# Span attention with joint small operations and exponentials by head

## The chip, the cores and the metric

The kernel runs on one core of a Trainium2 chip. The time is the device time of one execution in microseconds (us); lower is better. A profile of one execution shows what each engine did: TensorE (PE, with weight loads as PEld), VectorE (DVE), ScalarE (ACT), GpSimd (POOL) and SyncE (SP), which issues transfers.

## What is computed

A block of three layers, each added to its input. Batch 32, 64 rows each, width 256, 16 heads; the context has 1601 keys.

```
x = x + xattn(layernorm(x), ctx, ctx, mask, ...)      # 16 heads over 1601 keys
x = x + span(layernorm(x), W_span, W_val, W_out)
x = x + ffn(layernorm(x), ...)                        # shared gated part + 2 of 8 experts

def span(h, W_span, W_val, W_out):                    # per batch and head, m = 64 rows
    s, value = heads(h @ W_span.T, 2), heads(h @ W_val.T, 16)
    mean = sigmoid(s[..., 0]) * m
    soft = softplus(s[..., 1])
    diff = arange(m) - mean[..., None]
    attn = softmax(-soft[..., None] * diff * diff)    # over the 64 positions
    return merge(attn @ value) @ W_out.T
```

The change touches the span layer only, and there `mean`, `soft` and the softmax.

## The kernel before

**The large loop.** The cross attention takes nearly all of the time. It goes through 64 halves (a half is 8 heads of one batch element); half n has four quarters g, one for each group of key chunks. In a quarter PE makes the scores of the next half (line 495), projects keys (line 450, evicted by ACT at line 465) and values (line 450, evicted at line 482) of the next batch element, and in the first and last quarter multiplies probabilities by values (line 571). DVE evicts each bank of scores while it adds the mask (line 504), and keeps a running maximum in the PSUM tile `mrun` (line 525); ACT writes the first block into `mrun` (line 517, `first_maxima`), DVE reduces the turned maxima at line 539, once a half. POOL subtracts the maxima (line 556, four to a half), once ACT has copied them out (line 551); ACT takes the exponentials (line 561, four to a half). Scores, keys and values share six PSUM banks: a matmul that wants a bank waits for the eviction of what was in it.

**The order.** PE, DVE, ACT and POOL run in exactly the order in which the program writes the instructions (a manual schedule), each engine in order. SP's order is left to the framework. Quarter g of half n is stretch 4n + g.

**Small work between.** The other layers' work for a tile of 128 rows (two batch elements, four halves; 16 tiles) is cut into steps by generators. `run(stretch)` takes the step that is due, and what it yields is the number of stretches until the next. `run` stands after the quarter's scores and projections, and before `first_maxima` or the quarter's exponential. `WAITS` holds the yields of `span_steps` for tiles 0 to 13, `CLOSE` those for tiles 14 and 15, whose span layers reach into the end of the program, where feed-forward units fill PE.

**The span layer's steps** (`span_steps`, lines 213 to 356). After projections, z = exp(-|s|) for both columns of s. Then the small chain, lines 279 to 295, 20 operations on DVE over 128 x 16 elements. With z0 and z1 the two columns: the sigmoid is max(z0, [s0 >= 0]) / (1 + z0). The softplus is max(s1, 0) + log(1 + z1), the logarithm as 2 atanh(z1 / (z1 + 2)), by a series in odd powers up to the 15th, six Horner steps (lines 291 to 294). Its temporaries `num`, `den`, `rat`, `atp`, `acc` are `held`, slices of `mrun` (`aside`, line 400), so ACT's copy at line 517 comes after the chain; `rden`, `at`, `twice`, `at2`, `mean`, `soft` lie in SBUF. In the next steps, on `sc`, 128 x 16 heads x 64 positions: POOL subtracts the mean from the position (line 300), ACT squares (304), POOL multiplies by `soft` (305), DVE takes each head's minimum `least` (308), POOL subtracts it (309), ACT takes exp(-x) of all 1024 elements (311), DVE sums each head to `total` (313) and takes the reciprocal (314), POOL multiplies (315). PE transposes the result (323) for the product with the values, and the sum goes on to `x_kept` and the feed-forward part.

For tile t the chain runs in the first quarter of a half with n mod 4 = 2, `least` in its last quarter, the exponential in the first quarter of the next half, the sum in its second.

Of the kernel before, what the change touches and what calls it, by code (L numbers as in the profile page):

```python
# [15 lines left out]
F32 = mybir.dt.float32  # L16
U8 = mybir.dt.uint8
AF = mybir.ActivationFunctionType
ALU = mybir.AluOpType
AX = mybir.AxisListType  # L20
PSUM = bass.MemoryType.PSUM

P = 128
S = 64
D = 256
H = 16
# [6 lines left out]
GROUPS = [(0, 4), (4, 3), (7, 3), (10, 3)]  # L33
BETWEEN = [(), (1, 2, 3), (4, 5, 6), (7, 8, 9), (10, 11, 12)]
LN_EPS = 1e-5
MASKED = -1e30
BIG = 3e38
E, TOPK, PRIME, HASH_OFF = 8, 2, 11, 7919
# [23 lines left out]
def shape_constants() -> np.ndarray:  # L62
# [5 lines left out]
    for e in range(2):  # L68
        c[:, C_OWN + e] = (row % 32) // 16 == e
    c[:, C_PAD] = np.where(row >= KEYS - (NKC - 1) * CHUNK, 2 * MASKED, 0.0)  # L70
    return c
# [3 lines left out]
def perceiver_kernel(ctx: ExitStack, tc: tile.TileContext, a: dict[str, bass.AP], out: bass.AP):  # L75
    nc = tc.nc
# [6 lines left out]
    const = ctx.enter_context(tc.tile_pool(name="const", bufs=1))  # L83
# [80 lines left out]

    neghalf = const.tile([P, 1], F32, name="neghalf")
    nc.gpsimd.memset(neghalf, -0.5)
    own4 = const.tile([P, 2], F32, name="own4")
    nc.vector.tensor_scalar(own4, own, 0.25, None, ALU.mult)

# [6 lines left out]
    def spread_of(src, name: str):  # L176
# [7 lines left out]
        ve = work.tile([P, 1], F32, tag="ve", bufs=4, name=f"ve_{name}")  # L184
        nc.vector.tensor_scalar(ve, mv[:, 1:2], LN_EPS, None, ALU.add)
        rstd = work.tile([P, 1], F32, tag="rstd", bufs=4, name=f"rstd_{name}")
# [3 lines left out]
    def normalised(src, spread, name: str):  # L190
        neg, rstd = spread
        xn = work.tile([P, D], F32, tag="xn", name=f"xn_{name}")
        nc.scalar.activation(xn, src, AF.Identity, bias=neg)
        nc.scalar.activation(xn, xn, AF.Copy, scale=rstd)
        return xn
# [11 lines left out]

    WAITS = (1, 1, 1, 1, 1, 1, 1, 1, 1, 1, 1, 3, 3, 1, 1, 1)  # L210
    CLOSE = (1, 1, 1, 1, 0, 2, 1, 1, 1, 1, 1, 2, 1, 1, 1, 1)

    def span_steps(t: int, oT):
        waits = iter(CLOSE if t >= NTILE - 2 else WAITS)
        x = xs[t]
# [8 lines left out]
        h = normalised(x, spread, f"h{t}")  # L224
# [12 lines left out]
        z = span_pool.tile([P, H, 2], F32, tag="z", name=f"z_{t}")  # L237
# [13 lines left out]
        for b in range(2):  # L251
            for c in range(2):
                for j in range(4):
                    e, i = divmod(j, 2)
# [13 lines left out]
        def small(tag: str):  # L268
            return span_pool.tile([P, H], F32, tag=tag, name=f"{tag}_{t}")
# [1 line left out]


        held = aside(f"held_{t}")
        num, den, rat, atp, acc = (held[:, i * H : (i + 1) * H] for i in range(5))
        s0, s1, z0, z1 = span[:, :, 0], span[:, :, 1], z[:, :, 0], z[:, :, 1]
        mean, soft, rden, at, twice, at2 = (
            small(n) for n in ("mean", "soft", "rden", "at", "twice", "at2")
        )
        nc.vector.tensor_scalar(rat, z1, 2.0, None, ALU.add)
        nc.vector.tensor_scalar(den, z0, 1.0, None, ALU.add)  # L280
        nc.vector.tensor_scalar(num, s0, 0.0, None, ALU.is_ge)
        nc.vector.reciprocal(rat, rat)
        nc.vector.reciprocal(rden, den)
        nc.vector.tensor_tensor(num, z0, num, ALU.max)
        nc.vector.tensor_tensor(atp, z1, rat, ALU.mult)
        nc.vector.tensor_tensor(at, z1, rat, ALU.mult)
        nc.vector.scalar_tensor_tensor(twice, z1, 2.0, rat, ALU.mult, ALU.mult)
        nc.vector.tensor_tensor(at2, at, atp, ALU.mult)
        nc.vector.scalar_tensor_tensor(mean, num, float(S), rden, ALU.mult, ALU.mult)

        nc.vector.tensor_scalar(acc, at2, 1.0 / 15, None, ALU.mult)
        for n in (13, 11, 9, 7, 5, 3):
            nc.vector.scalar_tensor_tensor(acc, acc, 1.0 / n, at2, ALU.add, ALU.mult)  # L293
        nc.vector.scalar_tensor_tensor(acc, acc, 1.0, twice, ALU.add, ALU.mult)
        nc.vector.scalar_tensor_tensor(soft, s1, 0.0, acc, ALU.max, ALU.add)  # L295
        yield next(waits)
# [1 line left out]
        full = [P, H, S]  # L298
        sc = span_pool.tile(full, F32, tag="sc", name=f"sc_{t}")
# [6 lines left out]
        yield next(waits)  # L306
        least, total = small("least"), small("total")
        nc.vector.tensor_reduce(least, sc, AX.X, ALU.min)  # L308
        nc.gpsimd.tensor_tensor(sc, sc, least[:, :, None].to_broadcast(full), ALU.subtract)
        yield next(waits)  # L310
        nc.scalar.activation(sc, sc, AF.Exp, scale=-1.0)
        yield next(waits)
        nc.vector.tensor_reduce(total, sc, AX.X, ALU.add)  # L313
        nc.vector.reciprocal(total, total)
        nc.gpsimd.tensor_tensor(sc, sc, total[:, :, None].to_broadcast(full), ALU.mult)
        yield next(waits)
# [2 lines left out]
        for q in range(2):  # L319
            ps = mm_bank(f"psa_{t}_{q}")  # L320
            for i in range(4):
                n = 4 * q + i
# [6 lines left out]
        for c in range(2):  # L329
            for b in range(2):  # L330
                for j in range(4):
                    n = 4 * c + j
# [32 lines left out]
    madd = big.tile([P, NKC, S], F32, name="madd", bufs=1)  # L365
    nc.vector.tensor_scalar(madd[:CHUNK], m8[:CHUNK], -MASKED, MASKED, ALU.mult, ALU.add)
    nc.vector.tensor_scalar(
# [271 lines left out]
    def finish_steps(b: int, stretch: int):  # L639

        t = b // 2
        if b % 2 == 0:
            oT[t] = work.tile([P, 2, 2, S], F32, tag="oT", name=f"oT_{t}")
        flat = "p c u r q -> p (c u r q)"
        nc.vector.transpose(turned_pvs.rearrange(flat), pvs.rearrange(flat))
        by_head = turned_pvs.rearrange("p c u r i -> p (c u r) i")
        rec = work.tile([P, 8], F32, tag="rec", name=f"rec_{b}")
        nc.vector.reciprocal(rec, by_head[:, :, DK])
        o = work.tile([P, 8, DK], F32, tag="o", name=f"o_{b}")
        nc.vector.tensor_tensor(  # L650
            o, by_head[:, :, :DK], rec[:, :, None].to_broadcast([P, 8, DK]), ALU.mult
        )
        nc.vector.transpose(oT[t][:, :, b % 2, :], o.rearrange("p (c n) i -> p c (n i)", c=2))
        if b % 2:
            agenda[stretch + 1].append(span_steps(t, oT.pop(t)))
        yield
# [266 lines left out]
```

## Time and profile before

| | us |
|---|---|
| median of 4 runs | 1606.19 |
| lowest and highest | 1604.48, 1607.47 |
| the profiled execution | 1606.7 |
| its span, first to last instruction | 1604.7 |

The granted clock of TensorE was 0.997 over the span. Some groups of the span layer, each 16 times in the program, once for a tile (the mean of one in us), and beside them the large loop's:

| line | engine | what | us each |
|---|---|---|---|
| 279 to 295 | DVE | the small chain, 20 operations | 0.16 to 0.27 each |
| 300, 305, 309, 315 | POOL | operations on 128 x 1024 | 1.90 |
| 308, 313 | DVE | minimum, sum over 128 x 1024 | 1.20, 1.21 |
| 304, 311 | ACT | square, exponential of 128 x 1024 | 1.05, 1.07 |
| 504 | DVE | eviction of scores, 16 to a half | 0.58 |
| 525 | DVE | running maximum, 11 to a half | 0.69 |
| 556 | POOL | subtraction of the maxima | 3.73 |
| 561 | ACT | exponential of 124 x 1664 | 1.59 |

How to read it: a busy share counts only executing instructions. A row of a timeline has the start in us from the span's beginning, how long it took, engine, line, operation, what it writes and reads, shape and count, and in brackets how long the engine had stood idle before it and what ended that. Neighbours on an engine may overlap by about a tenth of a microsecond, as an instruction's record ends when its writes are in.

### The profile page before, as it was taken

How to read it: one execution, taken by the hardware profiler on the slowest of the kernel's cores; microseconds unless marked ns; L12 is line 12 of the kernel's file. 1: busy time of each engine (PE TensorE's matmuls, PEld its weight loads, DVE VectorE, ACT ScalarE, POOL GpSimd, SP SyncE). 2: the span in 40 equal slices, each digit the busy share in tenths (PEclk: the TensorE clock that was granted, in tenths of full speed). 3: DMA queues.
4: the chain of work that ended last, by engine and by line, in shares of the span. 5: the costliest groups of instructions: out<-in, count | busy, mean ns of one | idle time of the engine just before them, and what ended most of it. 6: DMA issues, size and time to landing. Idle time of an engine off the chain costs nothing.

```text
span 1604.7 us, 62733 instructions
## 1 busy us (share of the span) xinstructions
PE 1531.8 (95%) x28600; PEld 1101.7 (69%) x28600; DVE 1261.3 (79%) x2700; ACT 897.1 (56%) x1229; POOL 1121.1 (70%) x424
## 2 busy tenths in 40 slices
PE   8999999999999999999999999999999999988899
PEld 5676676676767676676766676676767676654487
DVE  4888888888888988888888888888888988885200
ACT  3565656565565656555666556555656556555311
POOL 1777777778687877788686877688686977771610
PEclk9999999999999999999999999999999999999999
DMA  5111111111111111111111111111111111004100
GB/s 170 56 40 35 38 44 38 34 50 44 50 44 50 31 41 34 34 49 44 50 44 50 31 41 36 39 44 44 50 44 50 32 44 36 15 2 152 56 23 30
DMA packets 52072, 73.78 MB, mean 46 GB/s; under 512 B 3812, under 2 KB 51040, under 8 KB 51680
## 3 DMA queue, kind: packets, MB, share of 16 engines
q1 hardware_dynamic: 50992, 69.00, 15.1%
q8 instruction: 224, 3.67, 1.0%
q10 hardware_dynamic: 816, 0.79, 0.1%
q14 instruction: 40, 0.33, 0.1%
HBM read 65.57 MB, written 4.19 MB: 43 GB/s over the span
## 4 chain that ended last, share of the span: by engine, by line
PE 60%; DVE 36%; issue 2%; ACT 1%; DMA 1%; POOL 1%; ACTq 0%; SPq 0%; DVEq 0%; POOLq 0%
PE pv L450 13%; PE pk L450 13%; DVE mrun L525 13%; DVE prob L504 13%; PE pvs L571 9%; PE psc L495 9%; PE py L853 3%; PE u L600 3%; PE pm L532 2%; PE ph L835 2%; PE pb L547 1%; DVE total L313 1%; DVE least L308 1%; DVE mrun L293 1%; PE po L343 1%
## 5 line engine op out<-in xcount | busy, mean ns | idle before, releaser
L556 POOL TENSOR_TENSOR prob<-prob,mb 124x1664 f32<-124x1664 f32 x252 | 936.1, 3733 | 305.6 <-ACT mb L551 210.3
L504 DVE TENSOR_TENSOR prob<-psc,madd 124x384 f32<-124x384 f32 (+1 forms) x1024 | 582.4, 582 | 176.1 <-PE psc L495 176.0
L525 DVE TENSOR_TENSOR mrun<-prob,mrun 124x512 f32<-124x512 f32 x704 | 483.9, 687 | 6.6 <-ACT mrun L517 2.6
L450 PE MATMUL pk<-ct,wkT_sb 128*32 128x361 f32 (+2 forms) x1768 | 405.0, 499 | 15.2 <-DMA wkT_sb<-in_wkT 5.6
L561 ACT ACTIVATE prob<-prob 124x1664 f32<-124x1664 f32 x256 | 403.1, 1587 | 16.9 <-POOL prob L556 14.0
L450 PE MATMUL pv<-wvT_sb,ct 128*32 128x256 f32 (+3 forms) x4268 | 385.8, 379 | 0.0
L450 PEld LDWEIGHTS pv<-wvT_sb,ct 128*32 128x32 f32 (+3 forms) x4268 | 258.5, 123 | 128.8 <-issue 13.8
L495 PE MATMUL psc<-qbd,kT 32*124 32x128 f32 x6656 | 303.1, 287 | 29.4 <-DVE prob L504 23.8
L495 PEld LDWEIGHTS psc<-qbd,kT 32*124 32x124 f32 x6656 | 239.8, 181 | 95.8 <-DVE prob L504 49.0
L465 ACT ACTIVATE kT<-pk,cols 128x372 f32<-128x372 f32 (+2 forms) x256 | 152.1, 594 | 273.1 <-PE pk L450 273.0
L450 PEld LDWEIGHTS pk<-ct,wkT_sb 128*32 128x32 f32 (+1 forms) x1768 | 158.5, 145 | 127.4 <-issue 53.3
L482 ACT COPY v<-pv 124x512 f32<-124x512 f32 (+1 forms) x224 | 124.7, 557 | 215.4 <-PE pv L450 215.0
L571 PE MATMUL pvs<-prob,v 124*17 124x64 f32 x13312 | 212.3, 220 | 1.1 <-issue 1.1
L571 PEld LDWEIGHTS pvs<-prob,v 124*17 124x17 f32 x13312 | 195.6, 98 | 21.1 <-issue 10.9
L517 ACT COPY mrun<-prob 124x512 f32<-124x512 f32 x64 | 38.6, 602 | 59.3 <-DVE soft L295 56.2
L855 DVE SCALAR_TENSOR_TENSOR ot<-py,prob 128x256 f32<-128x256 f32 x16 | 6.8, 425 | 75.7 <-PE py L853 75.7
L600 PE MATMUL u<-xfT,sw_sb 128*128 128x512 f32 x128 | 59.7, 616 | 1.3 <-ACT vbd L262 0.9
L547 PEld LDWEIGHTS pb<-cst,mc 128*124 128x124 f32 x256 | 28.9, 136 | 36.7 <-DVE mc L539 29.2
L532 PE MATMUL pm<-cst,mx 124*128 124x124 f32 x256 | 40.7, 281 | 11.7 <-DVE mx L525 11.6
L525 DVE TENSOR_TENSOR mx<-prob,mrun 124x512 f32<-124x512 f32 x64 | 43.9, 687 | 2.2
L842 ACT ACTIVATE hT<-ph,cols 128x256 f32<-128x256 f32 x32 | 13.4, 470 | 56.3 <-PE ph L835 56.3
L600 PEld LDWEIGHTS u<-xfT,sw_sb 128*128 128x128 f32 x128 | 24.3, 196 | 29.5 <-issue 24.8
(126 smaller groups left out, 1139.6 us busy)
## 6 DMA issues: line engine op xcount, KB each, us to landing
ct<-in_ctxT SPq DMA_DIRECT2D x64, 372.0 KB, 3.2
ct<-in_ctxT SPq DMA_DIRECT2D x32, 496.0 KB, 3.6
ct<-in_ctxT SPq DMA_DIRECT2D x32, 361.0 KB, 3.1
w<-in_w SPq DMA_DIRECT2D x16, 256.0 KB, 6.1
x<-in_x SPq DMA_DIRECT2D x16, 128.0 KB, 2.2
x_kept<-x SPq DMA_DIRECT2D x16, 128.0 KB, 2.3
prob<-x_kept SPq DMA_DIRECT2D x8, 256.0 KB, 5.4
out<-ot SPq DMA_DIRECT2D x16, 128.0 KB, 1.9
```

The lines of the kernel that those rows point to most:

```text
L450: nc.tensor.matmul(out[at:end], lhsT=lhsT[:, at:end], rhs=rhs, start=start, stop=stop, **(dict(tile_position=(0, at)) if tiled else {}),)
L465: nc.scalar.activation(kTs[c][:, k0 : k0 + kn], ps[:, :kn], AF.Identity, bias=cols[:, B_K + c : B_K + c + 1])
L482: nc.scalar.copy(vs[b % 2][:kn, 2 * u : 2 * u + n, :, :DK], ps[:kn, : n * D].rearrange("p (n h d) -> p n h d", n=n, d=DK),)
L495: nc.tensor.matmul(ps[:CHUNK, k * P : (k + 1) * P], lhsT=kTs[c][32 * j : 32 * j + 32, at : at + CHUNK], rhs=qbd[b // 2][32 * j : 32 * j + ...
L504: nc.vector.tensor_tensor(pair_of(n, j)[:, c0 : c0 + nb, :].rearrange("p k (e q) -> p k e q", e=2), ps[:CHUNK, : nb * P].rearrange("p (k e ...
L525: nc.vector.tensor_tensor(dst, block_of(n, k), run, ALU.max)
L532: nc.tensor.transpose(ps[:, j * CHUNK : (j + 1) * CHUNK], m[:CHUNK, j, :], ident[:CHUNK, :CHUNK])
L556: engine.tensor_tensor(sj, sj, m[:CHUNK, j, None, :].to_broadcast([CHUNK, NKC, P]), ALU.subtract)
L561: nc.scalar.activation(pair_of(n, j), pair_of(n, j), AF.Exp)
L571: nc.tensor.matmul(pvs[32 * j : 32 * j + DK + 1, c, :, r, :], lhsT=v[:kn, k, 8 * c + h, :], rhs=pair_of(n, h // 2)[:kn, k, (h % 2) * S : ( ...
L600: nc.tensor.matmul(ps, lhsT=w[:, c, hc * P : (hc + 1) * P], rhs=xfT[:, c, :, slot], start=(c == 0), stop=(c == 1),)
L853: nc.tensor.matmul(py, lhsT=x, rhs=w, start=(n == 0), stop=(n == len(terms) - 1))
```

## The change

- **The small chain** becomes 15 operations. A constant `one_two` (128 x 16 x 2: ones and twos, written by two memsets on POOL at the start) is added to z in one operation, one reciprocal over 32 elements gives both 1/(1 + z0) and 1/(2 + z1). Of the two copies of the ratio one goes (its square is made from `twice` and `atp`). The series has five fitted coefficients, `ATANH`, in place of seven terms: four Horner steps, not six. `num` is in SBUF now.
- **The softmax**: POOL's subtraction of the minimum goes. The exponential is taken head by head, 16 instructions of 128 x 64 elements, with the head's minimum as the bias of each partition, and each adds up its own output into `total` (`accum_out`). DVE's sum goes.
- **The steps**: the exponentials are two steps of eight heads each, so there are 17 yields. For tiles 0 to 13 the first eight are where the one exponential was (ahead of ACT's copy of line 517), the other eight a quarter later (ahead of the exponential of line 561); the reciprocal and POOL's product come a quarter later than before, and all after that stays in its quarter. For tiles 14 and 15 a yield of 0 puts both halves into the same stretch, where the one exponential was.
- PE's order is unchanged. On SP the store of tile 14's `x_kept` stands seven weight loads later in the queue.

```diff
+ATANH = (0.33333338, 0.19999444, 0.14308298, 0.1071537, 0.12144779)
...
+    one_two = const.tile([P, H, 2], F32, name="one_two")
+    for n in range(2):
+        nc.gpsimd.memset(one_two[:, :, n], float(n + 1))
...
-    WAITS = (1, 1, 1, 1, 1, 1, 1, 1, 1, 1, 1, 3, 3, 1, 1, 1)
-    CLOSE = (1, 1, 1, 1, 0, 2, 1, 1, 1, 1, 1, 2, 1, 1, 1, 1)
+    WAITS = (1, 1, 1, 1, 1, 1, 1, 1, 1, 1, 1, 1, 2, 3, 1, 1, 1)
+    CLOSE = (1, 1, 1, 1, 0, 2, 1, 1, 1, 1, 0, 1, 2, 1, 1, 1, 1)
...
-        num, den, rat, atp, acc = (held[:, i * H : (i + 1) * H] for i in range(5))
+        over = held[:, : 2 * H].rearrange("p (h k) -> p h k", k=2)
+        ge, atp, acc = (held[:, i * H : (i + 1) * H] for i in range(2, 5))
...
-        nc.vector.tensor_scalar(rat, z1, 2.0, None, ALU.add)
-        nc.vector.tensor_scalar(den, z0, 1.0, None, ALU.add)
-        nc.vector.tensor_scalar(num, s0, 0.0, None, ALU.is_ge)
-        nc.vector.reciprocal(rat, rat)
-        nc.vector.reciprocal(rden, den)
-        nc.vector.tensor_tensor(num, z0, num, ALU.max)
-        nc.vector.tensor_tensor(atp, z1, rat, ALU.mult)
-        nc.vector.tensor_tensor(at, z1, rat, ALU.mult)
-        nc.vector.scalar_tensor_tensor(twice, z1, 2.0, rat, ALU.mult, ALU.mult)
-        nc.vector.tensor_tensor(at2, at, atp, ALU.mult)
-        nc.vector.scalar_tensor_tensor(mean, num, float(S), rden, ALU.mult, ALU.mult)
-        nc.vector.tensor_scalar(acc, at2, 1.0 / 15, None, ALU.mult)
-        for n in (13, 11, 9, 7, 5, 3):
-            nc.vector.scalar_tensor_tensor(acc, acc, 1.0 / n, at2, ALU.add, ALU.mult)
+        nc.vector.tensor_tensor(over, z, one_two, ALU.add)
+        nc.vector.tensor_scalar(ge, s0, 0.0, None, ALU.is_ge)
+        nc.vector.reciprocal(over, over)
+        nc.vector.tensor_tensor(num, z0, ge, ALU.max)
+        nc.vector.tensor_tensor(atp, z1, over[:, :, 1], ALU.mult)
+        nc.vector.scalar_tensor_tensor(twice, z1, 2.0, over[:, :, 1], ALU.mult, ALU.mult)
+        nc.vector.scalar_tensor_tensor(mean, num, float(S), over[:, :, 0], ALU.mult, ALU.mult)
+        nc.vector.scalar_tensor_tensor(at2, twice, 0.5, atp, ALU.mult, ALU.mult)
+        nc.vector.tensor_scalar(acc, at2, ATANH[-1], None, ALU.mult)
+        for a in ATANH[-2::-1]:
+            nc.vector.scalar_tensor_tensor(acc, acc, a, at2, ALU.add, ALU.mult)
...
         nc.vector.tensor_reduce(least, sc, AX.X, ALU.min)
-        nc.gpsimd.tensor_tensor(sc, sc, least[:, :, None].to_broadcast(full), ALU.subtract)
-        yield next(waits)
-        nc.scalar.activation(sc, sc, AF.Exp, scale=-1.0)
-        yield next(waits)
-        nc.vector.tensor_reduce(total, sc, AX.X, ALU.add)
+        yield next(waits)
+        for part in range(2):
+            for h in range(part * H // 2, (part + 1) * H // 2):
+                nc.scalar.activation(
+                    sc[:, h, :], sc[:, h, :], AF.Exp, bias=least[:, h : h + 1], scale=-1.0,
+                    accum_out=total[:, h : h + 1],
+                )
+            yield next(waits)
         nc.vector.reciprocal(total, total)
```

More of the change, by code (lines that the diff above doesn't have):

```diff
@@ L273, in span_steps @@
         held = aside(f"held_{t}")
-        num, den, rat, atp, acc = (held[:, i * H : (i + 1) * H] for i in range(5))
+        over = held[:, : 2 * H].rearrange("p (h k) -> p h k", k=2)
+        ge, atp, acc = (held[:, i * H : (i + 1) * H] for i in range(2, 5))
         s0, s1, z0, z1 = span[:, :, 0], span[:, :, 1], z[:, :, 0], z[:, :, 1]
[L276 to L279, printed above, removed]
-        nc.vector.tensor_scalar(den, z0, 1.0, None, ALU.add)
-        nc.vector.tensor_scalar(num, s0, 0.0, None, ALU.is_ge)
-        nc.vector.reciprocal(rat, rat)
-        nc.vector.reciprocal(rden, den)
-        nc.vector.tensor_tensor(num, z0, num, ALU.max)
-        nc.vector.tensor_tensor(atp, z1, rat, ALU.mult)
-        nc.vector.tensor_tensor(at, z1, rat, ALU.mult)
-        nc.vector.scalar_tensor_tensor(twice, z1, 2.0, rat, ALU.mult, ALU.mult)
-        nc.vector.tensor_tensor(at2, at, atp, ALU.mult)
-        nc.vector.scalar_tensor_tensor(mean, num, float(S), rden, ALU.mult, ALU.mult)
-        nc.vector.tensor_scalar(acc, at2, 1.0 / 15, None, ALU.mult)
-        for n in (13, 11, 9, 7, 5, 3):
-            nc.vector.scalar_tensor_tensor(acc, acc, 1.0 / n, at2, ALU.add, ALU.mult)
+        mean, soft, num, twice, at2 = (small(n) for n in ("mean", "soft", "num", "twice", "at2"))
+        nc.vector.tensor_tensor(over, z, one_two, ALU.add)
[9 more added lines that the diff above has]
+            nc.vector.scalar_tensor_tensor(acc, acc, a, at2, ALU.add, ALU.mult)
         nc.vector.scalar_tensor_tensor(acc, acc, 1.0, twice, ALU.add, ALU.mult)
```

## The prediction

> **What bounds the kernel now.** I read the page first: busy shares and the chain that ended last.
>
> ```profile
> PE 1531.8 (95%) x28600; PEld 1101.7 (69%) x28600; DVE 1261.3 (79%) x2700; ACT 897.1 (56%) x1229; POOL 1121.1 (70%) x424
> PE 60%; DVE 36%; issue 2%; ACT 1%; DMA 1%; POOL 1%; ACTq 0%; SPq 0%; DVEq 0%; POOLq 0%
> ```
>
> TensorE (PE) is nearly full, yet a third of the chain runs over VectorE (DVE). A share of the chain is no saving: the chain turns to DVE wherever PE waited a tenth of a microsecond. So next came the busy time by half batch. A tile has four halves, each from one reduction of line 539 to the next; I call them A to D. These are C and D of a middle tile (columns after the length: busy time of PE, weight loads, DVE, ACT, POOL).
>
> ```profile
> core 0: us, PE busy (x) PEld busy (x) DVE busy (x) ACT busy (x) POOL busy (x), PEclk, DMA share, GB/s
> ...
> 792.09:815.04 22.95, 20.95 (x431) 14.99 (x430) 22.04 (x57) 13.96 (x19) 20.74 (x8) 1.00 0.01 2
> 815.04:835.90 20.86, 20.58 (x415) 14.48 (x414) 17.51 (x32) 12.57 (x16) 17.00 (x6) 1.00 0.29 80
> ```
>
> Half C is DVE's: DVE is idle 0.91 us of 22.95, PE 2.00. Half D is PE's: idle 0.28. The small chain (lines 279 to 295) and `least` lie in C; the exponential and `total` lie in D. The waits of PE in C say who holds it:
>
> ```profile
> PE psc L495 <- DVE prob L504: 1.1, 2, 0.6
> PE pm L532 <- DVE mx L525: 0.6, 1, 0.6
> ```
>
> All of it is DVE. Then DVE's timeline through C:
>
> ```profile
> 794.20 0.17 DVE L279 TENSOR_SCALAR mrun<-z 128x16 f32<-128x16 f32 x1
> ...
> 798.07 0.17 DVE L295 SCALAR_TENSOR_TENSOR soft<-span,mrun 128x16 f32<-128x16 f32 x1
> 798.16 0.55 DVE L504 TENSOR_TENSOR prob<-psc,madd 124x384 f32<-124x384 f32 x1
> 810.67 1.20 DVE L308 TENSOR_REDUCE least<-sc 128x16 f32<-128x1024 f32 x1
> ```
>
> The reader is to see that the first eviction of the next quarter (L504) starts the moment the chain lets go: 798.16 - 794.20 = 3.96 us for 20 operations, with no gap after them. ACT's timeline through D, and PE's third group of scores there:
>
> ```profile
> 817.43 1.07 ACT L311 ACTIVATE sc<-sc 128x1024 f32<-128x1024 f32 x1
> 818.39 0.60 ACT L517 COPY mrun<-prob 124x512 f32<-124x512 f32 x1
> ...
> 822.92 1.59 ACT L561 ACTIVATE prob<-prob 124x1664 f32<-124x1664 f32 x1
> 824.76 0.57 ACT L465 ACTIVATE kT<-pk,cols 128x372 f32<-128x372 f32 x1 [0.24 <-PE pk L450]
> ```
> ```profile
> 826.38 1.54 PE L495 MATMUL psc<-qbd,kT 32*124 32x128 f32 x24
> ```
>
> The other score groups of D take 0.93 us; this one takes 1.54, as its fourth bank comes only at 827.00 from DVE, and the keys behind it wait 0.15 more: about 0.77 us of D is DVE's, more than the idle time shows.
>
> **The small chain, DVE, half C.** Steps from start to start in the old chain: an operation that writes PSUM (`mrun`) 0.21 us, one that writes SBUF and whose result isn't wanted next 0.09 to 0.12, a reciprocal of 16 elements 0.30, a Horner step 0.217 (1.30 for six). The new chain: the joint addition over 32 elements 0.23; `ge` 0.21; one reciprocal over 32 elements 0.42 (8 elements take 207 ns at L648, 16 take 266 at L282: 7.4 ns an element, so 16 more add 0.12); `num` 0.09; `atp` 0.21; `twice` 0.12; `mean` 0.10; `at2` 0.21; `acc` 0.21; four Horner steps 0.87; the last two 0.31. Sum 2.98, saving 0.98 us. `num` and the squared argument moving from PSUM to SBUF is in these steps. DVE is continuous, so everything behind shifts, up to `least`: it reads what POOL leaves at 807.87 + 1.92 = 809.79 (L305), and POOL, which starts the half at the copy of line 551, does not move. `least` can go from 810.67 to 809.83 only. I take -0.84 us a tile, for tiles 0 to 14; tile 15's chain runs beside units of the feed-forward part and gains nothing. Bounds: 0 (a wait I don't see) to -0.98.
>
> **POOL's subtraction (L309) goes.** 1.90 us a tile, but POOL then stands idle 2.25 us until the copy of line 551 at 817.62: worth nothing in tiles 0 to 14. In tile 15 it is on the path. The two memsets of the new constant lie where POOL waits 9.6 us for its first load (98 ns for such a memset at L166).
>
> **`total` goes from DVE, half D.** 1.21 us; the reciprocal (0.25) moves one quarter later, behind the third quarter's evictions. Worth at most the 0.77 us that DVE costs PE in D. The product by it on POOL moves behind the third subtraction of line 556: 817.62 + 3 x 3.70 + 1.90 = 830.6, before the transposes of 837.1.
>
> **The exponentials, ACT.** One instruction of 1.07 us becomes sixteen. Let T be the time of one, start to start. Rows:
>
> ```profile
> L246 ACT ACTIVATE z<-z 128x32 f32<-128x32 f32 x16 | 3.7, 232 | 0.0
> L193 ACT ACTIVATE xn_h<-x,neg_h 128x256 f32<-128x256 f32 x16 | 8.3, 520 | 0.3 <-DVE neg_h L183 0.3
> ```
>
> L311 and L246 give 0.842 ns an element above 205 ns. L193 has a bias per partition: 515 ns (mean of its rows) against 421 by that line, 94 more. So 64 elements with a bias: 205 + 54 + 94 = 353 ns; neighbours overlap 0.10 (L311 to L517: 1.07 long, 0.96 apart), which leaves 0.254 a piece. What reading out the sum costs no row shows. Lower end: nothing, T = 0.254. As an instruction of its own of next to no elements it lasts 206 ns: overlapped 0.106 (T = 0.36), not overlapped 0.206 (T = 0.46), and with the exponential not overlapping either T = 0.56, the upper end. I take the middle of the two inner cases, T = 0.41.
>
> The Trainium skill speaks against the cut: "VectorE: DVE Perf Modes", section "The TRN2 errata — SBUF-src ops pay a fixed extra latency per instruction", gives ScalarE 224 cycles an instruction beside one for each element and advises 512 elements or more. The trace agrees with its 205 ns. The same page, section "Two Vector instructions with no wait between them", counts a VectorE operation that writes out its accumulator as two instructions; whether ScalarE does so no run here shows. With the 186 ns less 93 of overlap that "ScalarE: Activation LUTs", section "What ACT_TABLE_LOAD costs", states, T would be an estimated 0.35 and the change +1.5 us.
>
> What waits behind them, half D:
> - First eight, from 817.43: the copy into `mrun` (L517) stands behind, and DVE's first maximum, at 819.72, needs it; DVE is in order. It becomes late by 817.43 + 8T + 0.60 + 0.03 - 819.72 = 8T - 1.66, at T = 0.41 by 1.62. The removed `total` gives that back to DVE only later.
> - Second eight, from 822.92: behind them the exponential of line 561 (1.50 to the next) and the eviction of keys (L465, 0.57), whose bank the third group's fourth score matrix takes: 822.92 + 8T + 1.50 + 0.57 + 0.06 against 827.00, that is 8T - 1.94, and the keys' 0.15 goes: **8T - 2.09 for half D**, no lower than -0.77. This is later than what the first eight cause, and contains it. At T = 0.41: +1.19. PE works through after that, so it stays. Tiles 0 to 13.
>
> **The tail**, where all sixteen run at once and PE waits for the result:
>
> ```profile
> 1459.40 1.09 PE L323 MATMUL psa<-cst,sc 128*128 128x128 f32 x8 [2.82 <-POOL sc L315]
> ...
> 1493.36 1.09 PE L323 MATMUL psa<-cst,sc 128*128 128x128 f32 x8 [2.56 <-POOL sc L315]
> ```
>
> Tile 14: from the exponential at 1454.72 to the transposes 4.68 us; then 16T + 0.40 (reciprocal and steps) + 1.95 (POOL): 16T - 2.33 = +4.23. Tile 15: from `least`'s end 1486.66 to the transposes 6.70; then 16T + 2.44: 16T - 4.26 = +2.30 (not below -2.56). On SP, tile 14's store of `x_kept` is moved past seven weight loads (0.5 us each to issue: four took 2.03): they start earlier, the store later, but the readers of `x_kept` wait for tile 15's store at 1499.18 anyway. Without that cover 3.5 us.
>
> **Sum:** 15 x -0.84 + 14 x (8T - 2.09) + (16T - 2.33) + (16T - 4.26) = 144T - 48.5 us; at T = 0.41, -12.6 + 16.7 + 4.2 + 2.3 = +10.5. The profiled execution took 1606.7 (span 1604.7 and 2.0 around it), 0.5 above the median 1606.2: 1617.2 like it, **1617** as a median. T = 0.337 is the point of no change.
>
> **Rivals.** Told from no change is what differs by 0.2%, 3.2 us, so T from 0.315 to 0.36 is "the same".
> - The sum costs nothing beside the exponential, T = 0.254: 36.6 - 48.5 = -11.9, 1594. For it: the data pass the engine anyway. Against it: the result must be written somewhere, and no instruction in the trace writes for free.
> - T near 0.34: 1606. For it: 0.36, the well-overlapped read, is close by.
> - Nothing overlaps, T = 0.56: +32.1, 1638. For it: an instruction that needs the one before starts late (L194 starts 0.10 after its predecessor's end).
> - ACT, 44% idle, absorbs it all in the tiles: only -0.84 and -0.77 count, with the tail at T = 0.41: -12.6 - 10.8 + 6.5 = -16.9, 1589. Against it: L517 has 0.7 us of slack, eight pieces take 3.3. It decides only where PE has banks in hand, and D shows none.
>
> **Numbers.** My case (T 0.36 to 0.50) 0.45, with its own range 1609 to 1630; nothing overlaps 0.15; near 0.34 0.15; free sum 0.20; absorbed 0.05. Faster 0.25, same 0.15, slower 0.60. The range reaches from just under the free sum nearly to the case without overlap: 1592 to 1636.
>
> **What would show it.** ACT: pieces near 0.41 us apart, and whether a second instruction stands beside each. DVE: L279's chain 3.0 us long. Half C near 22.1 us, half D near 22.0. In D a new wait of DVE's first maximum for ACT's copy into `mrun`, and of the scores for ACT. Tail: PE's two waits for POOL near 7 and 5 us. I am wrong if T is under 0.32, or if D stays at 20.9 with T at 0.4.

## The result, and the profile after

The changed kernel takes 1609.18 us (median of 36 runs, 1606.85 to 1614.81), the kernel before 1607.12 (58 runs, 1602.98 to 1611.02): a ratio of 1.0015 [1.0009, 1.0021], about 2.4 us more. By the bound of 0.2% that is no change. The profiled execution has a span of 1607.8 us against 1604.7. So little movement is the sum of two larger ones. Up to the last reduction of line 542 (line 539 before) the changed kernel gains 4.8 us, behind it, in the tail, it loses 7.9.

Busy shares and the chain that ended last, from the page of after:

```profile
PE 1540.3 (96%) x28600; PEld 1108.5 (69%) x28600; DVE 1234.1 (77%) x2604; ACT 961.6 (60%) x1725; POOL 1092.5 (68%) x410
PE 61%; DVE 23%; POOL 8%; ACT 5%; issue 2%; DMA 0%; POOLq 0%; DVEq 0%; ACTq 0%
```

DVE has 96 operations less and falls from 36% of the chain to 23%, but POOL and ACT take its place there. ACT has 496 more instructions, where sixteen for one in 16 tiles would make 240. The groups of line 312 say why (columns: busy us, mean ns of one, idle before):

```profile
L312 ACT ACTIVATE sc<-sc,least 128x64 f32<-128x64 f32 x256 | 85.3, 338 | 0.8 <-DVE least L308 0.8
L312 ACT ACTIVATION_READ_ACCUMULATOR sc<-sc,least 128x1 f32 x256 | 48.8, 191 | 0.0
```

Each exponential is followed by an instruction of its own that reads out its sum. ACT's timeline has the steps between them:

```profile
816.04 0.34 ACT L312 ACTIVATE sc<-sc,least 128x64 f32<-128x64 f32 x1
816.28 0.19 ACT L312 ACTIVATION_READ_ACCUMULATOR sc<-sc,least 128x1 f32 x1
816.37 0.34 ACT L312 ACTIVATE sc<-sc,least 128x64 f32<-128x64 f32 x1
```

The exponential takes 0.24 us to the next start, the read 0.09: **T is 0.331 us** start to start.

The same tile's halves C and D, after (busy time of PE, weight loads, DVE, ACT, POOL):

```profile
core 0: us, PE busy (x) PEld busy (x) DVE busy (x) ACT busy (x) POOL busy (x), PEclk, DMA share, GB/s
790.82:812.97 22.15, 20.88 (x431) 15.05 (x430) 21.36 (x51) 13.07 (x19) 19.23 (x7) 1.00 0.01 3
812.97:834.29 21.32, 21.02 (x415) 14.76 (x414) 16.54 (x31) 17.40 (x47) 16.67 (x5) 1.00 0.29 79
```

C went from 22.95 to 22.15 us, D from 20.86 to 21.32; the median over the middle tiles says the same, -0.79 and +0.46. DVE's timeline shows where both begin:

```profile
792.93 0.19 DVE L283 TENSOR_TENSOR mrun<-z,one_two 128x32 f32<-128x32 f32 x1
...
795.89 0.17 DVE L295 SCALAR_TENSOR_TENSOR soft<-span,mrun 128x16 f32<-128x16 f32 x1
795.98 0.55 DVE L507 TENSOR_TENSOR prob<-psc,madd 124x384 f32<-124x384 f32 x1
...
818.64 0.70 DVE L528 TENSOR_TENSOR mrun<-prob,mrun 124x512 f32<-124x512 f32 x1 [0.90 <-ACT mrun L520]
```

The chain lasts 795.98 - 792.93 = 3.05 us where it took 3.96. In D the first maximum now waits 0.90 us for ACT's copy, which stands behind eight pieces.

PE in the tail, after:

```profile
1457.47 1.97 PE L326 MATMUL psa<-cst,sc 128*128 128x128 f32 x8 [5.71 <-POOL sc L318]
...
1462.09 4.33 PE L603 MATMUL u<-xfT,sw_sb 128*128 128x512 f32 x8
...
1470.17 10.45 PE L603 MATMUL u<-xfT,sw_sb 128*128 128x512 f32 x20
...
1497.02 1.52 PE L326 MATMUL psa<-cst,sc 128*128 128x128 f32 x8 [3.68 <-POOL sc L318]
```

The two waits grew from 2.82 and 2.56 us. What stands behind them got longer as well: the same eight transposes took 1.09 us before and take 1.97, and the first two groups of `u` (matmuls of a feed-forward unit) took 3.70 and 8.75 before and take 4.33 and 10.45. These are their rows before:

```profile
1461.88 3.70 PE L600 MATMUL u<-xfT,sw_sb 128*128 128x512 f32 x8
...
1469.33 8.75 PE L600 MATMUL u<-xfT,sw_sb 128*128 128x512 f32 x20
```

Windows of 5 us behind tile 14's wait, after and then before (the column behind POOL is the granted clock):

```profile
1460.00:1465.00 5.00, 5.00 (x41) 2.61 (x40) 1.25 (x5) 1.36 (x4) 0.55 (x1) 0.66 1.10 350
```
```profile
1460.00:1465.00 5.00, 5.00 (x49) 2.85 (x48) 1.25 (x5) 2.46 (x5) 0.55 (x1) 1.00 0.87 303
```

After, TensorE runs at half clock in four stretches between 1439 and 1505 us: 3.4, 6.8, 3.4 and 6.8 us long; before in two, between 1444 and 1503 us, 3.4 and 6.8. So two things are open: whether the readout and the place of the pieces explain D, and whether the clock explains what the waits don't.

### The profile page after: what moved, and what is told of

It is laid out like the page before. It is cut to its first block, busy times and chain, and to the rows that moved or that the text cites. A ratio compares the mean times of both kernels' runs of the same rounds, so it can differ in the third digit from the quotient of the medians.

```text
span 1607.8 us, 63124 instructions
## 1 busy us (share of the span) xinstructions
PE 1540.3 (96%) x28600; PEld 1108.5 (69%) x28600; DVE 1234.1 (77%) x2604; ACT 961.6 (60%) x1725; POOL 1092.5 (68%) x410
## 4 chain that ended last, share of the span: by engine, by line
PE 61%; DVE 23%; POOL 8%; ACT 5%; issue 2%; DMA 0%; POOLq 0%; DVEq 0%; ACTq 0%
PE pv L453 15%; PE pk L453 15%; PE psc L498 9%; DVE mrun L528 8%; PE pvs L574 8%; DVE prob L507 7%; POOL prob L559 5%; PE py L856 3%; ACT sc L312 3%; PE u L603 3%; PE pm L535 2%; PE ph L838 2%; POOL sc L305 1%; DVE least L308 1%; POOL sc L300 1%
## 5 line engine op out<-in xcount | busy, mean ns | idle before, releaser
L528 DVE TENSOR_TENSOR mrun<-prob,mrun 124x512 f32<-124x512 f32 x704 | 483.9, 687 | 19.3 <-ACT mrun L520 15.4
L498 PE MATMUL psc<-qbd,kT 32*124 32x128 f32 x6656 | 310.0, 288 | 22.8 <-DVE prob L507 18.1
L498 PEld LDWEIGHTS psc<-qbd,kT 32*124 32x124 f32 x6656 | 244.2, 181 | 91.8 <-DVE prob L507 37.9
L312 ACT ACTIVATE sc<-sc,least 128x64 f32<-128x64 f32 x256 | 85.3, 338 | 0.8 <-DVE least L308 0.8
L312 ACT ACTIVATION_READ_ACCUMULATOR sc<-sc,least 128x1 f32 x256 | 48.8, 191 | 0.0
L318 POOL TENSOR_TENSOR sc<-sc,total 128x1024 f32<-128x1024 f32 x16 | 30.6, 1911 | 26.0 <-DVE total L317 26.0
```

The lines of the kernel that those rows point to most:

```text
L312: nc.scalar.activation(sc[:, h, :], sc[:, h, :], AF.Exp, bias=least[:, h : h + 1], scale=-1.0, accum_out=total[:, h : h + 1],)
L498: nc.tensor.matmul(ps[:CHUNK, k * P : (k + 1) * P], lhsT=kTs[c][32 * j : 32 * j + 32, at : at + CHUNK], rhs=qbd[b // 2][32 * j : 32 * j + ...
L528: nc.vector.tensor_tensor(dst, block_of(n, k), run, ALU.max)
```

## The experiments

All ratios are to the kernel before, run on the same chip; "C" and "D" are the medians of these halves over the middle tiles.

**The chain alone.** The new small chain, with the old softmax and the old `WAITS` and `CLOSE`.

```diff
+        nc.gpsimd.tensor_tensor(sc, sc, least[:, :, None].to_broadcast(full), ALU.subtract)
         yield next(waits)
...
+        nc.scalar.activation(sc, sc, AF.Exp, scale=-1.0)
+        yield next(waits)
+        nc.vector.tensor_reduce(total, sc, AX.X, ALU.add)
```

> The shorter chain alone; the softmax and its steps are as before. Theory (each part acts where its own engine binds): half C shrinks from 22.95 to about 22.15 us for tiles 0 to 14, half D stays at 20.86, the tail as before: about -12 us against before, ratio 0.9925. Rival (the trace's -0.79 in half C came from the subtraction or the sum that left, not from the chain): ratio 1.000 and half C at 22.95.

Measured: 1596.32 us, 0.9926 [0.9911, 0.9942]; C 22.17, D 20.86.

**The exponentials alone.** The new softmax and yields, with the old chain of 20 operations.

```diff
-        nc.vector.tensor_tensor(over, z, one_two, ALU.add)
...
+        nc.vector.tensor_scalar(rat, z1, 2.0, None, ALU.add)
+        nc.vector.tensor_scalar(den, z0, 1.0, None, ALU.add)
...
```

> The exponentials by head alone; the small chain is as before. Theory: half C stays near 22.95, half D goes from 20.86 to about 21.32 (14 tiles, +6.4 us), the tail +8: about +14 us against before, ratio 1.009. Rival (removing the sum pays for the exponentials, the tail is noise): within 0.2% of before.

Measured: 1624.30 us, 1.0095 [1.0077, 1.0113]; C 22.95, D 21.32. Half D of the two kernels, the chain alone and then the exponentials alone:

```profile
808.47:829.33 20.86, 20.58 (x415) 14.48 (x414) 17.52 (x33) 13.34 (x16) 17.86 (x6) 1.00 0.30 80
```
```profile
818.98:840.30 21.32, 21.02 (x415) 14.76 (x414) 16.54 (x31) 16.58 (x47) 16.64 (x5) 1.00 0.30 79
```

Each part moves its own half and leaves the other's where it was. The tail is 161.3 us long with the chain alone and 170.6 with the exponentials alone (before 161.4, after 169.3). By the ratios -11.9 and +15.3 us make +3.4, beside +2.4 for both together: the parts add up within the intervals, and the whole loss is the exponentials'.

**The old softmax in the tail.** Tiles 14 and 15 take the old softmax and the old `CLOSE`, the other tiles the new one.

```diff
+        if t >= NTILE - 2:
+            nc.vector.tensor_reduce(least, sc, AX.X, ALU.min)
+            nc.gpsimd.tensor_tensor(sc, sc, least[:, :, None].to_broadcast(full), ALU.subtract)
+            yield next(waits)
+            nc.scalar.activation(sc, sc, AF.Exp, scale=-1.0)
+            yield next(waits)
+            nc.vector.tensor_reduce(total, sc, AX.X, ALU.add)
+        else:
```

> Changed kernel, but tiles 14 and 15 take the one exponential, POOL's subtraction and DVE's sum as before. Theory (the tail costs 3.1 + 1.2 us of waiting and about 4 us of matmuls at half clock after it): about -8 us against the changed kernel, -5.5 against before, ratio 0.9965; PE's wait before the transposes of tile 14 back at 2.8 us. Rival (the tail's length is chance of the clock): ratio 1.0015 as the changed kernel, whatever that wait.

Measured: 1601.23 us, 0.9954 [0.9938, 0.9970]; C 22.16, D 21.32. The tail is 158.6 us long (after 169.3, before 161.4), with one stretch of half clock, 6.8 us long, about its beginning.

**No sum.** `accum_out` is left out, and the reciprocal reads `least`, so the softmax is not normalised.

```diff
-                    accum_out=total[:, h : h + 1],
...
-        nc.vector.reciprocal(total, total)
+        nc.vector.reciprocal(total, least)
```

> Changed kernel without the sum in the exponentials: their second output is left out, and the reciprocal is taken of the minimum, so the softmax is not normalised. Theory (reading out the sum costs 0.331 - 0.254 = 0.077 us a piece): pieces 0.254 us apart, half D 8 x 0.077 = 0.6 us shorter than the changed kernel's 21.32 (20.7), the tail 2.5 us shorter besides the clock: about -11 us against the changed kernel, ratio to before 0.9945. Rival (the reading overlaps entirely, the pieces are 0.33 apart for the pointer bias): no change against the changed kernel.

Measured: 1594.62 us, 0.9917 [0.9898, 0.9936]. ACT's timeline in half D, and that half's window:

```profile
809.69 1.29 ACT L312 ACTIVATE sc<-sc,least 128x64 f32<-128x64 f32 x5
810.88 0.57 ACT L519 COPY mrun<-prob 124x512 f32<-124x512 f32 x1
```
```profile
806.36:826.95 20.59, 20.45 (x415) 14.54 (x414) 16.54 (x32) 15.66 (x31) 16.68 (x5) 1.00 0.30 82
```

Five pieces and the step to the next instruction take 810.88 - 809.69 = 1.19 us, 0.239 each: 0.015 under the floor of 0.254 that the prediction had worked out from longer instructions. With the sum it is 0.331, so **reading out the sum costs 0.092 us a piece**, half of its 0.191. Half D is 0.28 us shorter than before; its formula 8T - 2.09 gives -0.18 at this T. The tail is back at 160.9 us. Against the changed kernel the ratios give 15.7 us less where 11 were expected; in its trace the pieces are shorter than expected, and of the four stretches of half clock two remain, each 3.4 us long.

**The first eight later.** They stand behind ACT's copy into `mrun`.

```diff
-    WAITS = (1, 1, 1, 1, 1, 1, 1, 1, 1, 1, 1, 1, 2, 3, 1, 1, 1)
+    WAITS = (1, 1, 1, 1, 1, 1, 1, 1, 1, 1.5, 0.5, 1, 2, 3, 1, 1, 1)
...
                 first_maxima(n + 1)
+                run(4 * n + 0.5)
```

> Changed kernel, with the first eight exponentials behind ACT's copy into mrun instead of ahead of it, in the same quarter. Theory of the prediction (the second eight bind half D and contain what the first eight cause): half D stays at 21.3 us, no change against the changed kernel, ratio to before 1.0015; only DVE's wait for mrun (0.90 us) goes. Rival (the first eight are what half D pays for): half D falls by 0.8 us to 20.5, 14 tiles, -11 us, ratio 0.995.

Measured: 1608.26 us, 1.0019 [1.0007, 1.0031]; D 21.32, to the hundredth what it was. DVE's waits for ACT's copy fell from 15.4 us in the program to 2.6, and in their place PE's list of waits shows:

```profile
PE psc L498 <- ACT kT L468: 11.8, 15, 0.8
```

In the changed kernel the same row is 0.5 us, once in the program. PE's timeline in a half D says where the wait lies:

```profile
824.59 0.91 PE L498 MATMUL psc<-qbd,kT 32*124 32x128 f32 x18 [0.81 <-ACT kT L468]
```

That is 0.8 us a tile, in the third group of scores, for the keys' eviction that stands behind the second eight and the exponential of line 564. The second eight set the length of D; what the first eight cost is contained in it.

**PE kept busy, too much and then less.** Matmuls that nothing reads fill PE's two waits for the softmax in the tail: 10 and 7 of them, then 5 and 3.

```diff
+        if t >= NTILE - 2:
+            idle = mm_bank(f"idle_{t}")
+            for _ in range(10 if t == NTILE - 2 else 7):
+                nc.tensor.matmul(idle, lhsT=wvalT[:, 0, :P], rhs=sw1[:, 0, :], start=True, stop=True)
```

> Changed kernel, with 10 and 7 matmuls of 128x512 whose result nobody reads put before the transposes of tiles 14 and 15, where TensorE waits 5.7 and 3.7 us; they take about 4.5 and 3.2 us at full clock and delay nothing. Theory (the wait is followed by matmuls at half clock, which cost about 4 us of the tail): the half clock after these two waits is gone or shorter, and the time falls by 3 to 5 us against the changed kernel, ratio to before 0.999, although the work grows. Rival (the half clock is chance, or costs nothing on the path): no change, 1.0015, or slower.

Measured: 1609.66 us, 1.0030 [1.0018, 1.0041]. A miss of the experiment's own making, seen in PE's timeline:

```profile
1451.23 8.85 PE L323 MATMUL idle<-sw_sb,wvalT_sb 128*128 128x512 f32 x20
1459.92 1.04 PE L330 MATMUL psa<-cst,sc 128*128 128x128 f32 x8
```

Ten matmuls have twenty records and take 0.88 us each, twice what had been reckoned. They outlasted the wait and pushed the transposes back, from 18.94 to 22.26 us behind the last reduction, so the run says nothing for or against the clock. With half as many:

> As e5, with 5 and 3 of the unread matmuls: in e5 each took 0.88 us, twice what was reckoned, and they pushed the transposes back by 3.3 and 2.2 us. These take 4.4 and 2.7 us and end before the waits of 5.7 and 3.7 us do. Theory (matmuls at half clock behind the waits cost about 4 us of the tail): from tile 14's transposes to the end of its last product 6 us, not 9; the time falls by 3 to 5 us against the changed kernel, ratio to before 0.998 to 1.000. Rival (the half clock costs nothing on the path): 1.002 as the changed kernel.

Measured: 1604.27 us, 0.9997 [0.9988, 1.0007], about 2.9 us under the changed kernel by the ratios, and the two intervals don't meet. PE's timeline:

```profile
1450.85 4.56 PE L323 MATMUL idle<-sw_sb,wvalT_sb 128*128 128x512 f32 x10
1455.86 1.09 PE L330 MATMUL psa<-cst,sc 128*128 128x128 f32 x8 [0.45 <-POOL sc L318]
...
1465.79 8.75 PE L607 MATMUL u<-xfT,sw_sb 128*128 128x512 f32 x20
...
1490.94 1.09 PE L330 MATMUL psa<-cst,sc 128*128 128x128 f32 x8 [1.10 <-POOL sc L318]
```

The transposes take 1.09 us again and `u` 8.75, and no half clock is left between the first wait and the end of the units. That the clock differs is not the chance of one execution: its mean over the span lies between 0.992 and 0.995 in all executions of the changed kernel, between 0.997 and 0.999 in the twelve of this one, and between 0.995 and 0.999 in the 51 of the kernel before that ran beside the experiments. Within one kernel, too, it goes with the time: of the 23 executions of before on one chip, the six at 0.995 have a median of 1607.28 us, the five at 0.998 one of 1602.51. The table splits the tail at the two groups of transposes (us from the last reduction of line 539 or 542 to the first, on to the second, on to the end; from the timelines):

| kernel | to tile 14's | to tile 15's | to the end | sum |
|---|---|---|---|---|
| before | 16.06 | 33.96 | 111.35 | 161.4 |
| after | 18.94 | 39.55 | 110.82 | 169.3 |
| old softmax in the tail | 16.06 | 33.95 | 108.62 | 158.6 |
| 10 and 7 matmuls | 22.26 | 38.87 | 108.59 | 169.7 |
| 5 and 3 matmuls | 19.15 | 35.08 | 109.96 | 164.2 |

With the clock full the second stretch is 1.12 us over before, which is the longer wait of tile 15 alone; after has 4.47 more on top. The third stretch shows that before already paid for half clock behind tile 15's wait: about 2.7 us, the difference to the kernel with the old softmax, whose waits are as long. In the first stretch the length of half clock makes no difference: it is 16.06 us with 3.4 us of half clock (before) and with 6.8 (old softmax in the tail). So the clock is a net 4 us of after's 7.9: 4.47, less the 0.53 by which after's third stretch is shorter than before's. The 5 and 3 matmuls gain less than the clock cost, and one reason is a wait for DVE in the third stretch that after does not have:

```profile
1514.28 7.17 PE L842 MATMUL ph<-xfT,w 128*128 128x256 f32 x32 [0.91 <-DVE prob L635]
```

**Heads in ACT's gaps.** A version that uses what was found. The new chain; in half D the heads go four, four, three, three, two to where ACT waits for PE: before and after the copy into `mrun`, behind two of the keys' evictions and behind an exponential of line 564 (574 in this version); tiles 14 and 15 keep the old softmax.

```diff
-    WAITS = (1, 1, 1, 1, 1, 1, 1, 1, 1, 1, 1, 1, 2, 3, 1, 1, 1)
-    CLOSE = (1, 1, 1, 1, 0, 2, 1, 1, 1, 1, 0, 1, 2, 1, 1, 1, 1)
+    WAITS = (1, 1, 1, 1, 1, 1, 1, 1, 1, 1, 0.5, 0.25, 1, 0.75, 0.5, 1, 3, 1, 1, 1)
+    CLOSE = (1, 1, 1, 1, 0, 2, 1, 1, 1, 1, 1, 2, 1, 1, 1, 1)
...
+            for heads in (4, 4, 3, 3, 2):
...
                 project(project_keys, c, g, g == 3)
+                run(4 * n + g - 0.25)
...
                 first_maxima(n + 1)
+                run(4 * n + 0.5)
...
                 exponentials(n, g - 1)
+                run(4 * n + g + 0.5)
```

> New chain; in tiles 0 to 13 the sixteen exponentials stand in ACT's idle stretches of half D (4 ahead of the copy into mrun, 4 behind it, 3 behind each of two evictions of keys, 2 behind an exponential), the reciprocal and POOL's product one quarter later; tiles 14 and 15 take the softmax of before. Theory (the sum's removal is worth up to 0.77 us of half D once nothing waits for ACT): half C 22.16, half D 20.1 to 20.5, 15 x -0.8 and 14 x -0.4 to -0.8, -17 to -23 us against before, ratio 0.986 to 0.989. Rival (sixteen pieces cost half D its gain wherever they stand): half D 20.9 or more, ratio 0.993 or more.

Measured: 1582.03 us, **0.9856 [0.9833, 0.9879]**, faster than both kernels; C 22.16, D 19.97. Half D and part of ACT's timeline in it:

```profile
803.09:823.06 19.97, 19.97 (x414) 14.16 (x413) 16.43 (x32) 17.53 (x47) 16.73 (x5) 1.00 0.30 85
```
```profile
806.82 0.58 ACT L530 COPY mrun<-prob 124x512 f32<-124x512 f32 x1
...
808.77 0.57 ACT L478 ACTIVATE kT<-pk,cols 128x372 f32<-128x372 f32 x1
...
810.98 1.59 ACT L574 ACTIVATE prob<-prob 124x1664 f32<-124x1664 f32 x1
```

ACT does the same 16 pieces with their reads, 17.53 us of work in 19.97, and PE is busy for the whole half. Between the three instructions shown lie the second four heads (from 807.33) and three more (from 809.24). In half D the cost of the pieces was not their sum but what stood behind them.

**Two additions to it.** The feed-forward units 1 and 2 begun two stretches earlier (`{2: (1, 2), ...}` for `{4: (1, 2), ...}`), and, in another run, unread matmuls in the last three waits (3, 2 and 2).

> As the kernel before this one, and the feed-forward units 1 and 2 (3.6 us of matmuls) are begun ahead of tile 14's transposes instead of behind them. Theory: they fill TensorE's 2.8 us wait there, -2.8 us and sometimes a stretch at half clock less, ratio 0.002 below the kernel before this one. Rival (the units' banks are wanted by the steps behind them, whose evictions come later): no change or slower.

> The kernel with the heads in ACT's gaps (e7), with 3, 2 and 2 unread matmuls of 0.88 us in TensorE's last three waits (3.6 us for the last maxima, 2.8 and 2.5 us for the transposes of tiles 14 and 15). Theory: the two stretches at half clock of 6.8 us each shrink, the time falls by 2 to 5 us against e7, ratio to before 0.983. Rival: no change against e7, 0.9856.

Measured: 1581.34 us, 0.9849 [0.9826, 0.9872], and 1580.59 us, 0.9848 [0.9834, 0.9861]. Neither can be told from the version they start from, though 2.8 us had been expected of the first and 2 to 5 of the second. With the unread matmuls the granted clock does rise, from between 0.995 and 0.998 to between 0.998 and 1.000, and in the profiled executions the tail is 1.5 us shorter; the runs are too few to show a difference of that size.

## Why the prediction was wrong in its size

**The small chain: right in the middle tiles.** Forecast 2.98 us and -0.84 in C; measured 3.05 and -0.79. Alone it is worth 11.9 us, against 15 x 0.84 = 12.6. Tile 14, which the forecast counted in, gained nothing: its half C took 22.52 us before and 22.51 after.

**What waits behind the pieces: right.** 8T - 2.09 gives +0.56 for D at the measured T; it is +0.46. The first eight's delay, 8T - 1.66 = 0.99, is 0.90 at the first maximum, and is contained in the second eight's, as the run with the first eight later shows. `total` and its reciprocal were worth at most 0.77 by the forecast; with the pieces out of the way D fell by 0.89.

**The step that failed: the price of a piece, T = 0.41.** The readout is an instruction of its own and overlaps its neighbours by half, which was the case 0.36; I had taken the middle between it and the case without overlap. Both terms were high: 0.254 for the bare piece is 0.239, 0.156 for the readout is 0.092. At 144T each 0.01 is 1.4 us, and 0.079 too much is 11.4. At T = 0.331 the prediction's own sum is -0.8 us, the rival "T near 0.34". Its sentence on "ScalarE: Activation LUTs" of the Trainium skill, section "What ACT_TABLE_LOAD costs", with an estimated T of 0.35, was nearer than my middle.

**The term that was missing: the clock in the tail.** The lengthened paths were right: at T = 0.331 the formulas give +2.97 and +1.04, and the table has +2.88 and, at full clock, +1.12. But the sum ended at the waits. What runs behind them at half clock adds about 4 us. The trace of before held it: behind tile 15's wait of 2.56 us the granted clock between 1495 and 1500 was 0.53, and `u` x8 took 5.41 us there instead of 3.70.

```profile
1495.00:1500.00 5.00, 4.09 (x32) 2.53 (x23) 2.46 (x7) 1.56 (x4) 0.00 (x0) 0.53 0.00 0
```
```profile
1498.48 5.41 PE L600 MATMUL u<-xfT,sw_sb 128*128 128x512 f32 x8
```

-0.8 and +4 make +3.2; the spans differ by 3.1. That these agree so closely is partly luck, as the parts differ more: summed over the tiles, C fell by 10.7 us where the forecast has 12.6, and D rose by 6.4 where 8T - 2.09 at the measured T makes 7.8.

So the sign came out right by luck: with the right T alone the sum is -0.8, and what made it positive was the clock, which the forecast didn't have. The forecast of slower at 1617 stood on the price of the pieces. The beginning, up to the first reduction, is 0.6 us shorter; why stays open. So does one more remainder: between the first and the last reduction the loop gained 4.2 us, while 15 x -0.79 + 14 x 0.46 is -5.4. A and B changed by 0.2 us in sum; the rest lies in C, where not every tile gained 0.79: tile 14 gained nothing, tile 2 0.08 us and tile 8 1.42.

## What to carry to other kernels

Where one instruction becomes sixteen on an engine that is idle 44% of the time, look at what stands directly behind each piece in that engine's order and who waits for it; the same pieces made half D 21.32 us long in two blocks of eight and 19.97 when put where the engine waits anyway, while before, with one exponential and DVE's sum, it was 20.86. Where the sum holds many times a price that no row shows, the range of the forecast is the range of that price, and a measurement of it alone is worth more than any other. When a wait of TensorE is made longer, look at the granted clock behind the waits that it already has.

## What the runs showed of the hardware

- ScalarE's `accum_out` is a second instruction: it lasts 0.191 us, and it added 0.092 us to the 0.239 from one 128x64 exponential's start to the next.
- TensorE ran at half clock in stretches of 3.4 and 6.8 us in the tail. Most began during or behind a wait of 2.56 to 5.9 us, but the one at 1470.2 us of after stood behind waits of 0.46 and 1.30 us only, and the same two waits in before were followed by none. The Trainium skill, "TensorE: Matmul & The Clock Gate", section "Part 1: The HAM clock gate (the "warmup" mystery)", names a free-running window of about 3.4 us, and half clock after an idle window. The lengths agree. The waits do not all: several that half clock followed are shorter than a window. That a wait of 2.56 us was followed by it in before, and one of 2.57 us with the old softmax in the tail was not, shows that the length of a wait alone doesn't decide; what does stays open.
- A 128x512 matmul in f32 has two records and took 0.88 us at full clock (ten in 8.85 us).
